# A third step for one product, its sums in places of their own, and idle passes on a constant

## The chip, the cores and the metric

The kernel runs on one core of a Trainium2 chip. The metric is the time of one execution in device microseconds (us), all in fp32. A profile is one execution recorded by the hardware. Engines: PE is TensorE (PEld its weight loads), DVE is VectorE, ACT is ScalarE, POOL is GpSimd, SP is SyncE (which here only issues DMAs).

## The reference

The input x is 8 sequences of 256 tokens with 1024 features. Two steps follow each other, each adding its result to x:

```
logits = x . Wr^T + 5 * onehot(language id)      # 8 experts
gates  = softmax over the two largest logits, 0 elsewhere
x = x + x . W^T + 2 * sum over experts e of gate_e * (x . A_e^T) . B_e^T    # rank 16
x = x + x . weight[adapter id of the sequence]^T                             # 1024 x 1024
```

The first step's base product x . W^T is 2048 tokens by 1024 by 1024. The second step is one 1024 x 1024 product for each sequence, with a weight chosen by its id.

## The kernel before

**Products by Winograd's scheme.** The base product is cut 2 x 2: features into halves of 512, outputs into halves of 512, tokens into halves of 1024. Seven block products named "1", "2", "5", "6", "3", "7", "4" (in the order in which they run) take the place of eight. Each block product is cut 2 x 2 again, into the products P1 to P7: sums S1 to S4 of weight blocks (128 x 512) and T1 to T4 of token blocks (128 x 1024) are made on DVE, and PE multiplies them. P1 and P6 collect in the PSUM tile A, P5 in B, P2 in X; P7 goes to A, P3 to B, P4 to A again. Such a product is four matmuls of 128 x 512.

**The third step.** Where `leaves` names them, P2, P3 or P4 are cut 2 x 2 once more (`third`, L439): seven matmuls of 128 x 256, and small sums r1 to r4 (128 x 128) and q1 to q4 (128 x 256) on DVE. Pieces 2, 3 and 4 collect straight in the product's own PSUM tile, pieces 1, 5, 6 and 7 in PSUM of their own, from where DVE takes them (`take`, L496) and adds them to the result. `place` says where the small sums lie: 0 is a pool of tiles, 1 and 2 are inside block 11 of x once it is dead, 3 is a stretch of the result block y12 that isn't in use yet.

**Product 2**, the one in question, has the third step for P2 and P4, not for P3. S4 and T4 overwrite S2 and T2, so they wait until PE has read these (P6). P3 (L821 and L823) is S4 times a block of x, added into B in two parts, with pieces of P4 between them.

**What sets the order.** The order is written out by hand for the opening and planned by `product` (L712) for the rest. The planner keeps two clocks, `now["pe"]` and `now["dve"]`, which it advances by estimated costs (`us`, L364: elements plus 66 over 960). Optional DVE steps wait in `queue` with the events that they need; `ahead` (L379) runs those that fit before a given time, `force` (L396) runs one that is needed now with all that stand before it. Each engine runs its instructions in the order in which they are issued, so a DVE step that stands earlier delays all later ones.

**Around the change.** After the opening (product 1), PE does 64 small matmuls, `project` (L251), 128 x 136: the down-projection and the logits of the second half of the tokens. DVE meanwhile makes the gates of the first half (`gating(0)`, L293: a chain of small steps over 128 x 64, in which most need the one before), multiplies them onto h, transposes the result (`turn`, L327) and sends it off: twelve DMAs on SP's queue and four copies on POOL, into `hg`. Then come S1, T1, the logits of one quarter, S2, T2, six small sums of P2 and S3, T3. POOL copies a few elements of hg (L1088, so that it waits for those DMAs) and then issues four DMAs that add x11 onto x12 and x12 onto x22. Product 2 follows, and while it runs DVE does the second half's gates, its turn, and S1, T1, S2, T2 of product 5.

**Opening.** PE begins with `WARM` idle matmuls of 128 x 128 (L592) on the identity matrix that POOL makes; their result isn't used. The first real matmuls (L601) need one 128-row piece each of W and x.

Of the kernel before, what the change touches and what calls it, by code (L numbers as in the profile page):

```python
# [16 lines left out]
P = 128  # L17
# [1 line left out]
LANG_BIAS = 5.0  # L19
SCALING = 2.0  # L20
NEG = -3.0e38
WARM = 6


@with_exitstack
def kernel(
# [31 lines left out]
    nc = tc.nc  # L58
    D = O = 1024
    E = NE  # L60
    ER = awT.shape[2] - E
# [8 lines left out]
    TQ = TH // 2  # L70
# [18 lines left out]
    def flat(blk):  # L89
        return blk.rearrange("p k n -> p (k n)")  # L90
# [144 lines left out]
    def minus(out_, x, y):  # L235
        tt(out_, x, y, ALU.subtract)
# [127 lines left out]
    def us(n):  # L364
        return (n + 66) / 960
# [73 lines left out]
    def third(key, leaf, lhs, rhs, place, what):  # L439

        ra = lambda i, j: lhs()[:, j, ts(i, P)]
        rb = lambda i, j: rhs()[:, i, ts(j, NQ)]
        n0, n1 = slice(0, NQ), slice(NQ, TQ)
        t, own = {}, {}
        at = {"r13": 0, "r2": P, "r4": 2 * P, "q13": 3 * P, "q2": 3 * P + NQ, "q4": 3 * P + 2 * NQ}
        me = f"{key}:L{leaf}"

        def op(name, tag, fn, x, y, what):  # L450
            width = P if name[0] == "r" else NQ

            def run():
                if place == 0:
                    t[name] = sub3.tile([P, width], F32, name=f"{name}_{key}{leaf}", tag=tag)
                elif place == 3:
                    t[name] = flat(yb["12"])[:, 2048 + at[tag] : 2048 + at[tag] + width]
                else:
                    t[name] = spare(1536 + (place - 1) * 1152 + at[tag], width)
                fn(t[name], *(t[v] if isinstance(v, str) else v() for v in (x, y)))  # L460

            return us(width), what, f"{me}.{name}", run

        A, B = (lambda i, j: lambda: ra(i, j)), (lambda i, j: lambda: rb(i, j))
        ops = [
            op("r1", "r13", add, A(1, 0), A(1, 1), what),
            op("q1", "q13", minus, B(0, 1), B(0, 0), what),
            op("r2", "r2", minus, "r1", A(0, 0), what),
            op("q2", "q2", minus, B(1, 1), "q1", what),
            op("r4", "r4", minus, A(0, 1), "r2", what),  # L470
            op("q4", "q4", minus, B(1, 0), "q2", what),
        ]
        ops3 = [
            op("r3", "r13", minus, A(0, 0), A(1, 0), (f"{me}.5", f"{me}.r2")),
            op("q3", "q13", minus, B(1, 1), B(0, 1), (f"{me}.5", f"{me}.q2")),
        ]

        def piece(n, acc=None, banks=None, fresh=False):
            if n in (1, 5):
                own[n] = (single(f"P{n}_{key}{leaf}", n // 5) if banks is None else banks[n // 5])[:, n0]  # L480
            for x in {3: ("r4",), 4: ("q4",), 5: ("r1", "q1"), 6: ("r2", "q2", "P1"), 7: ("r3", "q3", "P6")}.get(n, ()):
                force(f"{me}.{x}")
            out_, l, r = {
                1: lambda: (own[1], ra(0, 0), rb(0, 0)),
                2: lambda: (acc[:, 0, n0], ra(0, 1), rb(1, 0)),
                3: lambda: (acc[:, 0, n1], t["r4"], rb(1, 1)),
                4: lambda: (acc[:, 1, n0], ra(1, 1), t["q4"]),
                5: lambda: (own[5], t["r1"], t["q1"]),
                6: lambda: (own[1], t["r2"], t["q2"]),
                7: lambda: (own[1], t["r3"], t["q3"]),  # L490
            }[n]()
            nc.tensor.matmul(out_, lhsT=l, rhs=r, start=(n in (1, 5) or fresh and n in (2, 4)), stop=True, skip_group_check=True)  # L492
            now["pe"] += 0.432
            event(f"{me}.{n}", 0.2)

        def take(n, dest, base=None, sub=False):  # L496

            cut = lambda v: {1: v[:, 0, n0], 6: v[:, 0, n1], 5: v[:, :, n1]}[n]
            if n == 7:
                cut = lambda v: v[:, 1, :].rearrange("p (j n) -> p j n", j=2)  # L500
            src = own[5 if n == 5 else 1]
            if n in (5, 7):
                src = src.unsqueeze(1).to_broadcast([P, 2, NQ])
            evict(NQ if n in (1, 6) else TQ, cut(dest), src, None if base is None else cut(base), f"{me}.P{n}", sub)

        return ops, ops3, piece, take

    def make_subs(key, w, x, leaves=(), what=(), last=(), place=0, early=False):

# [11 lines left out]
        def op(name, fn, x, y, what):  # L523
# [10 lines left out]

            return us(2 * width), what, f"{key}.{name}", run

        late = [
            (us(2 * OQ), (f"{key}:P6",), f"{key}.s4", lambda: minus(t["s2"], a(0, 1), t["s2"])),
            (us(2 * TQ), (f"{key}:P6",), f"{key}.t4", lambda: minus(t["t2"], b(1, 0), t["t2"])),
        ]  # L540
        deep = {}
        if 2 in leaves:
            deep[2] = third(key, 2, lambda: a(0, 1), lambda: b(1, 0), 0, leaf2)
        if 3 in leaves:
            deep[3] = third(key, 3, lambda: t["s2"], lambda: b(1, 1), 1, (f"{key}:P6",))
        if 4 in leaves:
            deep[4] = third(key, 4, lambda: a(1, 1), lambda: t["t2"], 3 if early else 2, (f"{key}:P6",))
        subs[key] = (a, b, t, late, deep)
        return [
            op("s1", add, a(1, 0), a(1, 1), what),  # L550
# [37 lines left out]
    def opening(key, dest):  # L588


        idle = pair("idle", 2)
        for i in range(WARM):  # L592
            nc.tensor.matmul(idle[:, 0, :P], lhsT=ident, rhs=ident, start=True, stop=True)  # L593
        mm = multiply()
        ops = make_subs(key, "11", "11")
        sums_of = [ops[i][3] for i in range(6)]
# [46 lines left out]
        for o in ops3:  # L643
            vec(o[0], o[3], o[2])
        late[0][3]()
        next_leaf = third(key, 3, lambda: t["s2"], lambda: b(1, 1), 3, ())
        for o in next_leaf[0]:
            vec(o[0], o[3], o[2])
        late[1][3]()
# [25 lines left out]
        chunk(1)  # L675
        piece(6)
        out(6, q1, q1)
        next_leaf = third(key, 4, lambda: a(1, 1), lambda: t["t2"], 0, ())
        for o in next_leaf[0]:
            vec(o[0], o[3], o[2])  # L680
        chunk(2)
# [30 lines left out]
    def product(key, base, dest, lora=None, tokens=None, sub=False, joined=None):  # L712
# [22 lines left out]
        own = list(deep[2][1]) if 2 in deep else []  # L735
        own += late[:1] + (deep[3][0] if 3 in deep else []) + late[1:] + (deep[4][0] if 4 in deep else [])
        own += (deep[3][1] if 3 in deep else []) + (deep[4][1] if 4 in deep else [])
        rest = list(queue)
        queue[:] = [q for q in rest if q[2].startswith(key)] + own + [q for q in rest if not q[2].startswith(key)]
        A = new("A")  # L740
# [49 lines left out]
        join(3)  # L790
        if 4 in deep:
            _, _, piece4, take4 = deep[4]
            piece4(1)
            take4(1, at[2], old[2], sub)
        if 3 in deep:
            hold[0] = key
            _, _, piece, take = deep[3]
            force(f"{key}.X2")
            piece(1, banks=halves(X))
            take(1, at[1], at[1], sub)  # L800
            force(f"{key}.B5")
            mm(B, None, None, False, "d", 1, part=())
            piece(5, banks=halves(X))
            if 4 in deep:
                piece4(5)
            piece(6)
            take(6, at[1], at[1], sub)
            if 4 in deep:
                piece4(6)
                take4(6, at[2], old[2], sub)  # L810
            for n in (2, 3, 4):
                piece(n, B)
            piece(7)
            take(7, at[1], at[1], sub)
            take(5, at[1], at[1], sub)
            if 4 in deep:
                force(f"{key}.A7")
                mm(A, None, None, False, "1", 0, part=())
        elif 4 in deep:
            need("s4", "B5")  # L820
            mm(B, t["s2"], b(1, 1), False, "d", 1, ms=(0,))  # L821
            piece4(5)
            mm(B, t["s2"], b(1, 1), False, "d", 1, ms=(1,))  # L823
            piece4(6)
            take4(6, at[2], old[2], sub)
        else:
            need("s4", "B5")
            mm(B, t["s2"], b(1, 1), False, "d", 1)
        put(1, B, True, "B3")
        join(1)  # L830
        if 4 in deep:
            if 3 not in deep:
                force(f"{key}.A7")
                mm(A, None, None, False, "1", 0, part=())
            for n in (2, 3, 4):
                piece4(n, A)
            piece4(7)
            take4(7, at[2], old[2], sub)
            take4(5, at[2], at[2], sub)
            put(2, A, True, "A4")  # L840
        else:
            need("t4", "A7")
            mm(A, a(1, 1), t["t2"], False, "1", 0)
            put(2, A, name="A4")
        join(2)
        hold[0] = ""
# [221 lines left out]
    add_w("21", "22")  # L1068
    add_w("11", "21")
    done.clear()  # L1070
    now["pe"], now["dve"] = 0.0, 6.0
    event("S2", 16.0)
    after(0.4, lambda: take(0, 1))
    for i, (t, f) in enumerate(gating(0)):
        vec(t, f, "gates0")
    project(1, 0, halves(pair("ps_h_1_0", 2)))
    now["pe"] += 7.5
    subs2 = make_subs("2", "12", "21", (2, 4), early=True)
    run(subs2[:2])
    after(0.4, lambda: take(1, 0))  # L1080
    run(subs2[2:])
    project(1, 1, singles("ps_h_1_1"))
    now["pe"] += 7.5
    force("gates0")
    after(0.4, lambda: take(1, 1))

    landed = const.tile([ER, 4], F32, name="landed")
    nc.gpsimd.tensor_copy(landed, hg[0][:, :, 0, 0])  # L1088
# [107 lines left out]
```

## Time and profile before

| | |
|---|---|
| Median of 3 runs | 421.59 us (421.51 to 422.34) |
| The profiled execution's own time | 421.75 us |
| Its span, first to last instruction | 420.0 us |
| PE busy | 415.0 us, 99% |
| DVE busy | 307.7 us, 73% |
| POOL busy | 31.0 us, 7% |
| Product 2's first and next product's first matmul | 58.30 and 88.38 us |
| Last instructions' DMA issue | 416.97 us |

Times inside the profile count from the span's start. A row of a timeline has the start, the duration of the merged group, engine, line, operation, output and input names, shapes and count; in brackets stands how long the engine sat idle before it and what released it. One fp32 matmul leaves two records of PE and two of PEld, so x8 are four matmuls. A DVE row's duration is longer than the distance to the next row by about 0.08 us, because the next step begins while the last one drains.

### The profile page before, as it was taken

How to read it: one execution, taken by the hardware profiler on the slowest of the kernel's cores; microseconds unless marked ns; L12 is line 12 of the kernel's file. 1: busy time of each engine (PE TensorE's matmuls, PEld its weight loads, DVE VectorE, ACT ScalarE, POOL GpSimd, SP SyncE). 2: the span in 40 equal slices, each digit the busy share in tenths (PEclk: the TensorE clock that was granted, in tenths of full speed). 3: DMA queues.
4: the chain of work that ended last, by engine and by line, in shares of the span. 5: the costliest groups of instructions: out<-in, count | busy, mean ns of one | idle time of the engine just before them, and what ended most of it. 6: DMA issues, size and time to landing. Idle time of an engine off the chain costs nothing.

```text
span 420.0 us, 3774 instructions
## 1 busy us (share of the span) xinstructions
PE 415.0 (99%) x1314; PEld 231.2 (55%) x1314; DVE 307.7 (73%) x507; ACT 44.5 (11%) x75; POOL 31.0 (7%) x43
## 2 busy tenths in 40 slices
PE   8999999999999999999999999999999999999996
PEld 6679975455655556555565444444444444444574
DVE  1877688999668998999989876765657666665531
ACT  1120310122130000000000101010101101010110
POOL 2000232131011101102000000000000000000000
PEclk9999999999999999999999999999999999999999
DMA  8995567997992965938902492855568384640202
GB/s 287 381 395 243 103 127 146 205 184 229 244 225 28 193 194 95 247 61 157 336 8 100 162 334 105 282 215 204 206 202 293 113 316 171 234 166 2 100 0 100
DMA packets 22563, 77.61 MB, mean 185 GB/s; under 512 B 2064, under 2 KB 5136, under 8 KB 17552
## 3 DMA queue, kind: packets, MB, share of 16 engines
q1 hardware_dynamic: 16240, 59.66, 39.8%
q0 software_dynamic: 5056, 16.78, 21.7%
q10 hardware_dynamic: 1248, 0.93, 0.7%
q8 instruction: 10, 0.16, 0.2%
q14 instruction: 9, 0.07, 0.0%
HBM read 55.61 MB, written 8.39 MB: 152 GB/s over the span
## 4 chain that ended last, share of the span: by engine, by line
PE 99%; POOL 0%; ACT 0%; issue 0%; POOLq 0%
PE A L944 23%; PE A L576 19%; PE B L944 13%; PE B L576 11%; PE ps_h L259 7%; PE X L944 7%; PE P L492 6%; PE A_last L1011 3%; PE X L492 3%; PE X L576 3%; PE A L492 2%; PE B L492 2%; PE idle L593 1%; ACT z L1041 0%; PE ids_wide L620 0%
## 5 line engine op out<-in xcount | busy, mean ns | idle before, releaser
L576 PE MATMUL A<-t,s 128*128 128x512 f32 x112 | 50.3, 592 | 0.0
L944 PE MATMUL B<-x,x 128*128 128x512 f32 x96 | 43.2, 592 | 0.0
L944 PE MATMUL A<-w,x 128*128 128x512 f32 x88 | 39.6, 592 | 0.0
L944 PE MATMUL A<-w,y 128*128 128x512 f32 x88 | 39.1, 592 | 0.0
L259 PEld LDWEIGHTS ps_h<-y,x 128*128 128x128 f32 x256 | 31.7, 190 | 2.9 <-issue 2.5
L576 PEld LDWEIGHTS A<-t,s 128*128 128x128 f32 x112 | 21.2, 190 | 20.8 <-issue 20.1
L259 PE MATMUL ps_h<-y,x 128*128 128x136 f32 x256 | 31.9, 279 | 0.0
L230 DVE TENSOR_TENSOR y<-P,y 128x512 f32<-128x512 f32 (+1 forms) x41 | 23.3, 570 | 10.8 <-PE P L492 5.7
L944 PEld LDWEIGHTS B<-x,x 128*128 128x128 f32 x96 | 18.2, 190 | 22.1 <-issue 22.0
L230 DVE TENSOR_TENSOR w<-w,w 128x1024 f32<-128x1024 f32 x16 | 19.4, 1224 | 13.5 <-PE A L944 13.5
L944 PEld LDWEIGHTS A<-w,x 128*128 128x128 f32 x88 | 16.7, 190 | 21.0 <-issue 20.8
L944 PEld LDWEIGHTS A<-w,y 128*128 128x128 f32 x88 | 16.7, 190 | 20.6 <-issue 20.6
L576 PE MATMUL A<-x,w 128*128 128x512 f32 x56 | 25.3, 592 | 0.0
L230 DVE TENSOR_TENSOR y<-A,y 128x1024 f32<-128x1024 f32 x18 | 22.0, 1223 | 4.2 <-PE A L576 2.9
L230 DVE TENSOR_TENSOR x<-w,x 128x1024 f32<-128x1024 f32 (+1 forms) x13 | 11.1, 863 | 10.8 <-PE A L944 7.8
L227 ACT ACTIVATE z<-A 128x512 f32<-128x512 f32 x12 | 7.2, 597 | 101.0 <-PE A L944 101.0
L230 DVE TENSOR_TENSOR w<-x,w 128x1024 f32<-128x1024 f32 x8 | 9.7, 1224 | 10.2 <-PE A L944 5.7
L576 PEld LDWEIGHTS A<-x,w 128*128 128x128 f32 x56 | 10.4, 190 | 9.8 <-issue 9.6
L230 DVE TENSOR_TENSOR x<-x 128x1024 f32<-128x1024 f32 (+1 forms) x17 | 15.8, 947 | 0.0
L230 DVE TENSOR_TENSOR y<-X,y 128x256 f32<-128x256 f32 (+2 forms) x17 | 12.8, 752 | 3.8 <-PE X L492 3.3
L230 DVE TENSOR_TENSOR z<-z,X 128x512 f32<-128x512 f32 x7 | 4.8, 689 | 13.6 <-PE X L944 13.6
L944 PE MATMUL X<-w,y 128*128 128x512 f32 x32 | 14.4, 592 | 0.0
(200 smaller groups left out, 612.3 us busy)
## 6 DMA issues: line engine op xcount, KB each, us to landing
x<-w_dram SPq DMA_DIRECT2D x24, 1024.0 KB, 4.8
x<-xT_dram SPq DMA_DIRECT2D x10, 1024.0 KB, 11.8
w<-w_dram SPq DMA_DIRECT2D x8, 1024.0 KB, 4.8
out_dram<-z SPq DMA_DIRECT2D x15, 512.0 KB, 2.9
w<-w POOLq DMA_DIRECT2D x8, 512.0 KB, 5.3
x<-x POOLq DMA_DIRECT2D x4, 1024.0 KB, 9.8
x<-xT_dram POOLq DMA_DIRECT2D x4, 1024.0 KB, 11.4
y<-y POOLq DMA_DIRECT2D x8, 512.0 KB, 5.1
```

Of the source, the lines that this page charges most:

```text
L227: nc.scalar.activation(out_, x, AF.Copy, scale=scale)
L230: nc.vector.tensor_tensor(out_, x, y, op)
L259: nc.tensor.matmul(ps[v][:, u * EA : (u + 1) * EA], lhsT=xk(k, j, c)[:, ts(r, P)], rhs=aw_sb[:, k, :], start=(first and k == some[0] and u ...
L492: nc.tensor.matmul(out_, lhsT=l, rhs=r, start=(n in (1, 5) or fresh and n in (2, 4)), stop=True, skip_group_check=True)
L576: nc.tensor.matmul(acc[:, m, :], lhsT=l, rhs=r, start=(first and i < len(ms)), stop=(i >= len(steps) - len(ms)), skip_group_check=True,)
L593: nc.tensor.matmul(idle[:, 0, :P], lhsT=ident, rhs=ident, start=True, stop=True)
L944: nc.tensor.matmul(accs[name], lhsT=lhs[:, k // 2, k % 2, :], rhs=rhs[:, k, :], start=(first and k == 0), stop=(k == KH - 1), skip_group_c ...
L1011: nc.tensor.matmul(acc, lhsT=lhs[:, k // 2, k % 2, :], rhs=rhs[:, k, ts(v, m)], start=(first and k == 0), stop=(k == KH - 1), skip_group_c ...
```

## The change

The change has four parts.

1. Product 2 gets the third step for P3 too (`leaves` (2, 3, 4)). P3's piece 1 and piece 5 go to the two halves of X, after X has been read out.
2. Its S4 and T4 no longer overwrite S2 and T2: S4 lies in y12, T4 in y22 (`apart`). So they don't wait for P6, nor do P4's six small sums, and T4, these sums and S4 are now made ahead of the product, right after the last logits. P3's small sums get a new place 4, in gaps of y12.
3. P2's six small sums move from behind T2 to between the first steps of the first half's gates, one after each step. The second half's gates are no longer held back in the last part of product 2 (`hold` isn't set for it).
4. The idle matmuls read a constant 1.0 (one element for each partition, read over and over) that the program's preamble sets, and there are seven in place of six.

```diff
-WARM = 6
+WARM = 7
...
+                elif place == 4:
+                    to = {"r13": 3712, "r2": 3840, "r4": 3968, "q13": 1664, "q2": 0, "q4": NQ}[tag]
+                    t[name] = flat(yb["12"])[:, to : to + width]
...
-    def make_subs(key, w, x, leaves=(), what=(), last=(), place=0, early=False):
+    def make_subs(key, w, x, leaves=(), what=(), last=(), place=0, early=False, apart=None):
...
-        late = [
-            (us(2 * OQ), (f"{key}:P6",), f"{key}.s4", lambda: minus(t["s2"], a(0, 1), t["s2"])),
-            (us(2 * TQ), (f"{key}:P6",), f"{key}.t4", lambda: minus(t["t2"], b(1, 0), t["t2"])),
-        ]
+        def op4(name, x):
+
+            old, width = ("s2", OQ) if name == "s4" else ("t2", TQ)
+
+            def run():
+                if apart is None:
+                    t[name] = t[old]
+                else:
+                    t[name] = apart[name].rearrange("p (k n) -> p k n", k=2)
+                minus(t[name], x, t[old])
+
+            return us(2 * width), (f"{key}:P6",) if apart is None else (), f"{key}.{name}", run
+
+        late = [op4("s4", a(0, 1)), op4("t4", b(1, 0))]
+        what4 = (f"{key}:P6",) if apart is None else ()
...
-            deep[3] = third(key, 3, lambda: t["s2"], lambda: b(1, 1), 1, (f"{key}:P6",))
+            deep[3] = third(key, 3, lambda: t["s4"], lambda: b(1, 1), 4 if early else 1, what4)
...
-            deep[4] = third(key, 4, lambda: a(1, 1), lambda: t["t2"], 3 if early else 2, (f"{key}:P6",))
+            deep[4] = third(key, 4, lambda: a(1, 1), lambda: t["t4"], 3 if early else 2, what4)
...
+        one = nc.const_aps.tensor(1.0, [P, P])
         for i in range(WARM):
-            nc.tensor.matmul(idle[:, 0, :P], lhsT=ident, rhs=ident, start=True, stop=True)
+            nc.tensor.matmul(idle[:, 0, :P], lhsT=one, rhs=one, start=True, stop=True)
...
+        own = [q for q in own if q[2] not in done]
...
+            need("t4")
             piece4(1)
...
-            hold[0] = key
+            if key != "2":
+                hold[0] = key
             _, _, piece, take = deep[3]
-            force(f"{key}.X2")
+            need("s4", "X2")
             piece(1, banks=halves(X))
...
-    now["pe"], now["dve"] = 0.0, 6.0
+    now["pe"], now["dve"] = 0.0, 3.5
     event("S2", 16.0)
     after(0.4, lambda: take(0, 1))
-    for i, (t, f) in enumerate(gating(0)):
-        vec(t, f, "gates0")
     project(1, 0, halves(pair("ps_h_1_0", 2)))
     now["pe"] += 7.5
-    subs2 = make_subs("2", "12", "21", (2, 4), early=True)
+    apart2 = {"s4": flat(yb["12"])[:, 3200:3712], "t4": flat(yb["22"])[:, : C * ER]}
+    subs2 = make_subs("2", "12", "21", (2, 3, 4), early=True, apart=apart2)
+    small2, subs2[4:10] = subs2[4:10], []
+    for t, f in gating(0):
+        vec(min(t, 0.16) if t < 0.5 else t, f, "gates0")
+        run([small2.pop(0) for _ in small2[:1]])
     run(subs2[:2])
     after(0.4, lambda: take(1, 0))
     run(subs2[2:])
...
-    force("gates0")
     after(0.4, lambda: take(1, 1))
+    _, _, _, (s4, t4), deep2 = subs["2"]
+    run([t4] + deep2[4][0] + [s4])
```

The other products' calls only change the name under which S4 and T4 are found; they still lie on S2 and T2.

More of the change, by code (lines that the diff above doesn't have):

```diff
@@ L645, in opening @@
         late[0][3]()
-        next_leaf = third(key, 3, lambda: t["s2"], lambda: b(1, 1), 3, ())
+        next_leaf = third(key, 3, lambda: t["s4"], lambda: b(1, 1), 3, ())
         for o in next_leaf[0]:
@@ L677, in opening @@
         out(6, q1, q1)
-        next_leaf = third(key, 4, lambda: a(1, 1), lambda: t["t2"], 0, ())
+        next_leaf = third(key, 4, lambda: a(1, 1), lambda: t["t4"], 0, ())
         for o in next_leaf[0]:
@@ L820, in product @@
             need("s4", "B5")
-            mm(B, t["s2"], b(1, 1), False, "d", 1, ms=(0,))
+            mm(B, t["s4"], b(1, 1), False, "d", 1, ms=(0,))
             piece4(5)
-            mm(B, t["s2"], b(1, 1), False, "d", 1, ms=(1,))
+            mm(B, t["s4"], b(1, 1), False, "d", 1, ms=(1,))
             piece4(6)
@@ L827, in product @@
             need("s4", "B5")
-            mm(B, t["s2"], b(1, 1), False, "d", 1)
+            mm(B, t["s4"], b(1, 1), False, "d", 1)
         put(1, B, True, "B3")
@@ L842, in product @@
             need("t4", "A7")
-            mm(A, a(1, 1), t["t2"], False, "1", 0)
+            mm(A, a(1, 1), t["t4"], False, "1", 0)
             put(2, A, name="A4")
```

## The prediction

> **What bounds the kernel now.** I read the page's busy table and its chain first. In both, columns are engine, time and share.
>
> ```profile
> PE 415.0 (99%) x1314; PEld 231.2 (55%) x1314; DVE 307.7 (73%) x507; ACT 44.5 (11%) x75; POOL 31.0 (7%) x43
> ...
> PE 99%; POOL 0%; ACT 0%; issue 0%; POOLq 0%
> ```
>
> TensorE (PE) is busy for 415.0 of 420.0 us and carries the whole chain. So time goes only with matmuls removed, with a slow clock ended sooner, or with a PE wait removed; it comes only with a new PE wait. The view of PE's waits has a single line, at the very start:
>
> ```profile
> PE idle L593 <- POOL ident masks.py:199: 1.5, 1, 1.5
> ```
>
> Next, PE's timeline of the first ten us (start, duration, instruction, count; one fp32 matmul leaves two records), and the landing times of the two loads issued first, at 0.75 (last column: us from issue to landing):
>
> ```profile
> 1.53 2.93 PE L593 MATMUL idle<-ident 128*128 128x128 f32 x12 [1.53 <-POOL ident masks.py:199]
> ...
> 4.25 2.97 PE L576 MATMUL X<-x,w 128*128 128x512 f32 x4
> ...
> 7.06 1.09 PE L259 MATMUL ps_h<-y,x 128*128 128x136 f32 x8
> ...
> 7.98 1.88 PE L576 MATMUL X<-x,w 128*128 128x512 f32 x4
> ```
>
> ```profile
> x<-xT_dram SPq DMA_DIRECT2D x1, 256.0 KB, 3.1
> w<-w11T_dram ACTq DMA_DIRECT2D x1, 128.0 KB, 3.3
> ```
>
> The same two matmuls take 7.06-4.25 = 2.81 us at first and 9.70-7.98 = 1.72 us afterwards (the next group starts at 9.70): 1.09 us are lost to half speed. Half speed loses half its time, so it lasted some 2.2 us after 4.25, to about 6.43, which is 4.9 us after the first idle pass at 1.53. The two loads land at 0.75+3.1 = 3.85 and 0.75+3.3 = 4.05; the first real weight load starts at 4.06.
>
> Last, product 2 on PE, at the place of its P3 (78.92 and 81.93 are P3's four matmuls; P4's pieces stand between):
>
> ```profile
> 78.49 0.59 PE L492 MATMUL P<-t,w 128*128 128x256 f32 x2
> 78.92 1.88 PE L576 MATMUL B<-x,s 128*128 128x512 f32 x4
> 80.64 1.02 PE L576 MATMUL B<-hg,bdiff 128*128 128x512 f32 x2
> 81.50 0.59 PE L492 MATMUL P<-y 128*128 128x256 f32 x2
> 81.93 1.88 PE L576 MATMUL B<-x,s 128*128 128x512 f32 x4
> 83.64 1.02 PE L576 MATMUL B<-hg,bdiff 128*128 128x512 f32 x2
> ```
>
> **Part 1: P3 in seven pieces.** It removes four 128x512 matmuls, 1.72 (78.92 to 80.64) + 1.71 (81.93 to 83.64) = 3.43 us, and adds seven 128x256 ones at 0.433 (81.50 to 81.93) = 3.03 us. The low-rank matmuls stay. PE gains 0.40 us, if nothing waits.
>
> **Part 2: what it costs VectorE (DVE).** P3's pieces need eight small sums, 4 x (0.20+0.34) = 2.1 us, and four more reads out of PSUM, 0.33+0.33+0.73+0.64 = 2.0 us. DVE had room: it idles 1.95 us before 64.08, and 0.68 us twice more (before 68.02 and 75.26). The question is whether every step stays ahead of PE, so I lay the new order (as the built program has it) out with the start-to-start times of these rows: a 128x1024 step 1.14, 128x512 0.60, 128x256 0.34, 128x128 0.20; a gate step 0.26 when it needs the one before, 0.14 when it doesn't (two in 0.30 at 49.62).
>
> ```profile
> 49.62 0.30 DVE L230 TENSOR_TENSOR y<-y 128x64 f32<-128x64 f32 x2
> ...
> 61.90 0.24 DVE L230 TENSOR_TENSOR y<-ps_h,bias 128x16 f32<-128x16 f32 x2
> 64.08 0.42 DVE L230 TENSOR_TENSOR y<-P,y 128x256 f32<-128x256 f32 x1 [1.95 <-PE P L492]
> ```
>
> First gates: six steps took 1.55 (47.04 to 48.59); with a small sum between each they take 6 x 0.14 + 1.62 = 2.46. Up to T2 all is 0.9 us later; then the six small sums (1.61, 58.55 to 60.16) are missing, so the pair at 61.90 comes at 61.20 and DVE is free at 61.37. The 0.9 us delay is covered: S2 and T2, done at 59.6, are read on PE at 64.31. It also moves the first turn's twelve DMAs on SP and four copies on POOL, and behind them in POOL's queue the wait for their landing (65.06, now 66.0) and the four adds onto x12 and x22. PE first reads the turned gates at 69.90, 3.9 us later. The first add onto x12 landed before 73.1 (POOL issues the next one then), now 74.0; product 5's T1 reads it at 81.7 at the earliest. Nothing there costs time.
>
> From 61.37: T4 1.14, P4's six sums 1.62, S4 0.60 and 0.12 for its end: 64.84. Two sums of P3 0.54, the P1 read of P2 0.33, its r3 and q3 0.54, four sums of P3 1.08: 67.33. Seven second-gate steps 1.68, A6 1.14, a P6 read 0.33, gates up to the exponential and past it 1.35+0.53: 72.36. B5 1.14, four gate steps 0.73, gates onto h 1.14, P7 and P5 reads 1.45: 76.82. X2 1.14, the transpose 1.17, A7 1.14, P4's first read 0.33: 80.61, and P3's first read ends at 81.02. On PE, P3's first piece follows P4's at 78.92 and needs X2 (ends 78.05): no wait. After two low-rank matmuls P3's second piece is due at 81.07, and in the built order it waits for that read at 81.02: it just fits, with 0.05 us to spare. What hides all this is 0.05 us of slack; every 0.1 us that DVE is later there is 0.1 us on the end, and behind the waiting piece stands all of PE.
>
> Two costs are not in that sum. First, POOL's copies for the second turn:
>
> ```profile
> 83.38 3.07 POOL L338 COPY hg<-y 32x256 f32<-32x256 f32 x4 [4.40 <-DVE y L330]
> 83.41 0.64 DVE L230 TENSOR_TENSOR y<-t 128x256 f32<-128x256 f32 x1
> 83.97 0.88 DVE L230 TENSOR_TENSOR x<-w 128x512 f32<-128x512 f32 x1
> 84.77 1.41 DVE L230 TENSOR_TENSOR x<-x 128x1024 f32<-128x1024 f32 x1
> 86.11 0.41 DVE L230 TENSOR_TENSOR y<-P,y 128x256 f32<-128x256 f32 x1
> ```
>
> While POOL copies, a sum of two SBUF tiles is 0.2 us longer (1.41 for 1.22, 0.88 for 0.68); the read from PSUM at 86.11 is not. The copies now come at about 79.9 (behind the fourth add on POOL, 78.12 plus the 0.9 of delay and its 0.86) and cover product 5's S1 and T1: 80.94, 81.74, 83.08; then r3 0.20, two P6 reads 0.67 and q3, which ends at 84.36. PE's P7 of P3 waits for it and is due at 81.07 + 7 x 0.433 = 84.10: 0.26 us of stall; without contention q3 ends at 83.96 and there is none. Second, A7 and two reads from PSUM also lie beside these copies. The Trainium skill ("SBUF — State Buffer", "Who interferes with whom") says that a VectorE step with at most one SBUF input doesn't contend with GpSimd. The trace has only the small read at 86.11 for it, near the copies' end; should A7 and the reads be slower as the SBUF sums are (0.2 + 0.1 + 0.1), 0.4 us of stall follow. I take 0, with row and rule. Third, the exit: product 5's B is due at 92.24-0.40 = 91.84 and needs A4, which the same layout ends at 91.4 to 91.9: no more than what is counted. Part 2 costs 0.25, between 0 and 0.7. Parts 1 and 2: -0.15 us (-0.4 to +0.3).
>
> **Part 3: the idle passes.** They no longer wait for the identity (1.47), only for the engines' common start; DVE and SP begin at 0.75 to 0.83, so I take 0.85. Seven passes of 0.42 (the twelve records' starts) end at 3.8: the first real matmul stays bound by its load at 4.05. The gain is only in when full speed is granted. By the row, 4.9 us after the first pass: 5.75 for 6.43, worth 0.68/2 = 0.34 us. The Trainium skill speaks against taking that as fixed: "TensorE: Matmul & The Clock Gate" ("What's actually happening") has a free-running window of about 3.4 us at whose end a busy window opens the clock. By it, the grant comes 3.4 to 6.8 us after the first pass: half speed on real work costs 0.45 to 2.15 us before and 0.1 to 1.8 after; the mean gain is again 0.34, but one run may move by over 1 us either way. The times shown (421.51 to 422.34, 0.83 apart) look like that. I take the -0.34 of the row, and the spread of the rule for the range. With windows ending at 3.01 and 6.43 as in this profile, PE was busy for 1.5 us of the one that ends at 3.01, now 2.2: should that suffice, all 1.09 is gained. At the other end the grant stays where it is: 0.
>
> **Sum.** -0.15-0.34 = -0.5 us. The profiled execution took 421.75 (span 420.0 plus 1.75 around it), the median is 421.59: 421.25 and 421.1, so I say 421.2. A measurement tells about 0.2% (0.84 us) from no change, so the likeliest outcome is a gain too small to be told.
>
> **Rivals.** (a) The clock opens a window earlier, or DVE just fits everywhere: -0.4 to -0.15 and -1.09 make 420.1 to 420.5, and combinations of half of it end near 420.7. For it: the first window is now 64% busy. Against: 43% were not enough before. 0.30. (b) It doesn't do what it says: the grant stays and the stalls eat the 0.40: 421.5 to 421.8. 0.20. (c) Slower: DVE is late at P3's second piece. If small sums between gates don't fill the gaps (0.26 a gate step for 0.14: 0.7 us), and PSUM reads contend (0.4), the read ends at 82.1, PE stalls 1.05, and 0.25 more at P7: 421.7-0.4+1.3 = 422.6. From 0.4 us of lateness on, the change costs time. For it: a margin of 0.05 after 20 us of unbroken DVE work. Against: the step times repeat to 0.01 us. 0.12. The forecast has the other 0.38.
>
> **How the numbers follow.** Faster (below 420.75) is case (a), 0.30; slower (above 422.43) is (c), 0.12; same 0.58. The range, 420.3 to 422.1, takes in -1.3 (the early clock with a stall) and +0.4 (no clock gain, both contentions).
>
> **What would show it.** Right: idle passes from 0.85 with x14 records; the first X matmuls in 2.1 to 2.5 us rather than 2.81; seven 128x256 pairs of records in place of P3; DVE without idle from 61 to 91; at most one PE wait on DVE, under 0.3 us, at P3's P7. Wrong: a wait of 0.5 us or more at P3's second piece, a PE wait for DMA in the opening, a wait at product 5's B, or X matmuls as slow as before.

## The result and the profile after

The changed kernel takes 421.09 us (median of 22 runs, 420.25 to 421.55), the kernel before 421.62 us in as many runs beside it (420.77 to 422.44). The ratio is 0.9984, 95% interval 0.9978 to 0.9991: a gain of 0.4 to 0.9 us. It is clear of zero and, most likely, under 0.2%. The profiled execution took 421.29 us, with a span of 419.5 (421.75 and 420.0 before).

The page after, engines' busy time and the chain:

```profile
PE 415.3 (99%) x1322; PEld 232.7 (55%) x1322; DVE 310.1 (74%) x519; ACT 44.4 (11%) x75; POOL 29.6 (7%) x43
...
PE 99%; ACT 0%; issue 0%
```

PE is still the whole chain. Its busy time didn't fall, although P3 costs less: the idle passes now run for longer, and they count as busy. The view of PE's waits has again only the one at the start, which is now the engines' common start rather than the identity:

```profile
PE idle L608 <- PEq L1208: 0.8, 1, 0.8
```

PE's opening after (start, duration, group):

```profile
0.79 3.33 PE L608 MATMUL idle<-const-float32-1.0 128*128 128x128 f32 x14 [0.79 <-PEq L1208]
4.08 3.02 PE L590 MATMUL X<-x,w 128*128 128x512 f32 x4
6.94 1.09 PE L259 MATMUL ps_h<-y,x 128*128 128x136 f32 x8
```

The passes begin 0.74 us earlier, but the first two real matmuls take 6.94-4.08 = 2.86 us, as slow as before (2.81). In this one execution full speed was granted hardly earlier (at 6.21 us by the trace's record of the clock, 6.43 before); only the start moved. Product 2 after, from P3's first piece to the next product's first matmul:

```profile
78.80 0.59 PE L495 MATMUL X<-x,y 128*128 128x256 f32 x2
...
80.95 0.67 PE L495 MATMUL X<-y 128*128 128x256 f32 x2
81.46 0.59 PE L495 MATMUL P<-y 128*128 128x256 f32 x2
...
87.92 3.60 PE L590 MATMUL A<-x,w 128*128 128x512 f32 x8
```

Two pieces follow each other by 0.43 us everywhere but after 80.95, where it is 81.46-80.95 = 0.51: 0.08 us is waited at P3's second piece, the place that the prediction named. Product 2 takes 87.92-58.18 = 29.74 us, against 88.38-58.30 = 30.08: 0.34 us of gain. It also begins 58.30-58.18 = 0.12 us earlier. Together that is the whole difference of the two spans, because what follows product 5's first matmul takes 331.6 us in both (419.5-87.92, 420.0-88.38).

VectorE and POOL after: the first gates with P2's small sums between their steps, then the stretch from the last logits to product 5's sums:

```profile
46.92 0.22 DVE L286 TENSOR_REDUCE y<-y 128x8 f32<-128x64 f32 x1
47.06 0.28 DVE L230 TENSOR_TENSOR r<-w 128x128 f32<-128x128 f32 x1
...
61.10 0.24 DVE L230 TENSOR_TENSOR y<-ps_h,bias 128x16 f32<-128x16 f32 x2
...
79.02 1.19 DVE L230 TENSOR_TENSOR y<-A,y 128x1024 f32<-128x1024 f32 x1
...
80.46 0.41 DVE L230 TENSOR_TENSOR y<-X,y 128x256 f32<-128x256 f32 x1
80.79 0.67 DVE L230 TENSOR_TENSOR x<-w 128x512 f32<-128x512 f32 x1
81.38 1.22 DVE L230 TENSOR_TENSOR x<-x 128x1024 f32<-128x1024 f32 x1
```

```profile
79.16 1.69 POOL L338 COPY hg<-y 32x256 f32<-32x256 f32 x4
```

A gate step with a small sum behind it takes 47.06-46.92 = 0.14 us of VectorE's time, the forecast's figure. The logits' pair stands at 61.10 (61.90 before), and from there VectorE has no gap over 0.34 us. P3's first read ends at 80.87 and PE is due at 80.95: the fit that the layout promised (81.02 for 81.07, with everything 0.12 us earlier here), and yet PE waits 0.08 us. POOL's copies came at 79.16 and end at 80.85, just as S1 of product 5 (80.79) begins.

### The profile page after: what moved, and what is told of

The parts are those of the page before. It is cut to its first block, busy times and chain, and to the rows that moved or that the text cites. A ratio compares the mean times of both kernels' runs of the same rounds, so it can differ in the third digit from the quotient of the medians.

```text
span 419.5 us, 3804 instructions
## 1 busy us (share of the span) xinstructions
PE 415.3 (99%) x1322; PEld 232.7 (55%) x1322; DVE 310.1 (74%) x519; ACT 44.4 (11%) x75; POOL 29.6 (7%) x43
## 4 chain that ended last, share of the span: by engine, by line
PE 99%; ACT 0%; issue 0%
PE A L962 23%; PE A L590 19%; PE B L962 13%; PE B L590 10%; PE ps_h L259 7%; PE X L962 7%; PE P L495 6%; PE X L495 4%; PE A_last L1029 3%; PE X L590 3%; PE A L495 2%; PE B L495 2%; PE idle L608 1%; ACT z L1059 0%; PE ids_wide L635 0%
## 5 line engine op out<-in xcount | busy, mean ns | idle before, releaser
L230 DVE TENSOR_TENSOR y<-X,y 128x256 f32<-128x256 f32 (+2 forms) x21 | 15.0, 715 | 3.8 <-PE X L495 3.3
L962 PE MATMUL X<-x,y 128*128 128x512 f32 x32 | 14.4, 592 | 0.0
```

The costliest lines, as they stand in the source:

```text
L230: nc.vector.tensor_tensor(out_, x, y, op)
L962: nc.tensor.matmul(accs[name], lhsT=lhs[:, k // 2, k % 2, :], rhs=rhs[:, k, :], start=(first and k == 0), stop=(k == KH - 1), skip_group_c ...
```

## The experiments

My theory was the prediction's: P3's pieces give 0.40 us less what PE waits for VectorE, and the idle passes give about 0.34 us on average by an earlier grant of full speed, with a large scatter from run to run. The rivals were that one of the two carries everything, and that VectorE has room enough for the order not to matter. Ratios are to the kernel before, run on the same chip. It took 421.49 us (44 runs) beside the passes alone, the first measurement of P3 without the passes, the sums behind T2 and the last experiment, and 421.78 us (48 runs) beside the others, so compare ratios from one experiment to the next, not microseconds.

**The idle passes alone.** To the kernel before:

```diff
-WARM = 6
+WARM = 7
...
+        one = nc.const_aps.tensor(1.0, [P, P])
         for i in range(WARM):
-            nc.tensor.matmul(idle[:, 0, :P], lhsT=ident, rhs=ident, start=True, stop=True)
+            nc.tensor.matmul(idle[:, 0, :P], lhsT=one, rhs=one, start=True, stop=True)
```

> The kernel before with the idle passes of the change alone (seven, on the constant). Theory: the earlier passes open the clock earlier by their head start on average, 0.7 us, worth 0.34 us: ratio 0.9992 (0.9985 to 1.0000), single runs over 1 us apart. In the profile: passes from 0.79, no new wait on PE, product 2's first matmul at 57.7 to 58.6. Rival (the profile of the changed kernel, where the grant came only 0.22 us earlier): 0.11 us, ratio 0.9997. Rival (all of the gain is P3): 1.0000.

Measured: 421.07 us in 13 runs, ratio 0.9991 (0.9983 to 0.9999). So the passes give some time. How much, the interval leaves open: it holds the theory's 0.34 us and the rival's 0.11. PE's opening in this kernel's profile:

```profile
4.13 2.02 PE L576 MATMUL X<-x,w 128*128 128x512 f32 x4
6.00 1.09 PE L259 MATMUL ps_h<-y,x 128*128 128x136 f32 x8
```

Here the two matmuls take 1.87 us rather than 2.86: nearly all of the half speed was over before real work began. From product 2's to product 5's first matmul it is 87.32-57.24 = 30.08 us, as before.

**P3 without the passes.** To the changed kernel, the passes of before (six, on the identity).

> The changed kernel with the idle passes of before (six, on the identity). Theory: only P3's seven pieces are left, 0.40 us less the 0.08 us of wait at P3's second piece: 0.32 us under the kernel before, ratio 0.9992. From product 2's first to product 5's first matmul: 29.74 us, as in the changed kernel (30.08 before). Rival (P3 carries the whole measured gain): 0.67 us, ratio 0.9984. Rival (the idle passes carry all): 1.0000.

Measured: 421.43 us in 14 runs, ratio 0.9997 (0.9988 to 1.0006), which holds both the theory and "nothing". The profile has product 2 at 87.91-58.24 = 29.67 us. A second measurement of the same kernel, with more runs:

> The changed kernel with the old idle passes, once more with five rounds, because the first measurement (ratio 0.9997, 0.9988 to 1.0006) couldn't tell the theory from its rival. Theory: what its profile shows in product 2 (29.67 us for 30.08) is all there is, 0.40 us, ratio 0.9990. Rival (product 2's gain is given back later): 1.0000.

Measured: 421.34 us in 22 runs, ratio 0.9988 (0.9982 to 0.9995). The two measurements, weighed by their intervals, make about 0.9991 (0.9986 to 0.9996; an estimate of mine), some 0.4 us. The profiles settle it: product 2 takes 29.68 us in this one too (88.80-59.12), and what follows product 5's first matmul takes 331.58 to 331.61 us in all profiles of this document but that of P3's pieces alone. So P3's pieces give time of their own, and "given back later" falls. The opening of this second profile is the slowest of all that have idle passes:

```profile
4.42 3.63 PE L590 MATMUL X<-x,w 128*128 128x512 f32 x4
7.88 1.09 PE L259 MATMUL ps_h<-y,x 128*128 128x136 f32 x8
```

The two matmuls take 3.46 us, although the passes stand where they stood before.

**No idle pass at all.** To the changed kernel, `WARM = 0`.

> The changed kernel without any idle pass. Theory (a window of 3.4 us at a free phase, so a grant 3.4 to 6.8 us after PE's first work, and here that is the first real matmul at 4.05): half speed lasts 3.4 to 6.8 us of real work and costs 1.7 to 3.4 us, against 0.1 to 1.7 with the passes: slower than the changed kernel by about 1.6 us, 422.7, ratio to the kernel before 1.0025 (1.0015 to 1.004). Rival (the grant comes near 6 us whatever PE did before, as four of the profiles have it at 5.7 to 6.4): no change against the changed kernel, ratio 0.9985.

Measured: 422.63 us in 17 runs, ratio 1.0022 (1.0014 to 1.0029). By the ratios that is 1.6 us over the changed kernel (0.9984). The theory's figure holds, the fixed moment falls. The first matmul waits for its load and then four records take 3.78 us where 1.88 is the full pace:

```profile
4.36 3.78 PE L590 MATMUL X<-x,w 128*128 128x512 f32 x4 [4.36 <-DMA w<-w11T_dram]
```

**The small sums behind T2.** To the changed kernel:

```diff
-    small2, subs2[4:10] = subs2[4:10], []
+    small2 = []
```

> The changed kernel with product 2's six small sums back behind T2 instead of between the first gates. Theory: VectorE reaches T4 0.7 us later (six gate steps at 0.26 for 0.14) and nothing gives that back, so the wait at P3's second piece grows from 0.08 to 0.6 to 0.8 us: slower than the changed kernel by 0.5 to 0.7, that is 421.7, ratio to the kernel before 1.0000 (0.9995 to 1.0008). Rival (the 0.7 us are absorbed in gaps of VectorE before 81, at A6, B5 or the exponential): no more than 0.2 us over the changed kernel, ratio 0.9987.

Measured: 421.81 us in 13 runs, ratio 1.0007 (0.9999 to 1.0016). PE now waits long enough for VectorE that its timeline marks it:

```profile
79.03 1.88 PE L590 MATMUL B<-hg,bdiff 128*128 128x512 f32 x4
81.40 0.70 PE L495 MATMUL X<-y 128*128 128x256 f32 x2 [0.49 <-DVE y L230]
81.93 0.59 PE L495 MATMUL P<-y 128*128 128x256 f32 x2
```

The piece was due at 79.03+1.72 = 80.75, and the next one starts at 81.93, so it began to stream at 81.50: 0.75 us of wait (the row's 0.49 leaves out the time until the group before is modelled to end). Product 2 takes 88.40-57.98 = 30.42 us, 0.68 more than with the sums between the gates. T4 begins 0.67 us later, counted from product 2's first matmul (61.74-57.98 for 61.27-58.18), and nothing on VectorE gave that back; without this move P3's pieces cost more than they save.

**S4 and T4 in place.** To the changed kernel:

```diff
-    subs2 = make_subs("2", "12", "21", (2, 3, 4), early=True, apart=apart2)
+    subs2 = make_subs("2", "12", "21", (2, 3, 4), early=True)
...
-    _, _, _, (s4, t4), deep2 = subs["2"]
-    run([t4] + deep2[4][0] + [s4])
```

> The changed kernel with S4, T4 and P4's sums back on S2 and T2 and behind P6 (P3's seven pieces, the sums between the gates and the idle passes stay). Theory: VectorE's gap at 62 to 64 us is filled by the second gates instead, which don't have to wait, so only dependent gate steps (0.26 for 0.14) and one wait are lost: the wait at P3's second piece is 0.3 to 0.5 us instead of 0.08, product 2 takes 30.0 to 30.2 us, time 421.3 to 421.5, ratio to the kernel before 0.9992. Rival (S4 and T4 behind P6 leave the gap unused and cost its 1.95 us): 422.9, ratio 1.0035.

Measured: 421.43 us in 13 runs, ratio 0.9996 (0.9988 to 1.0004). Product 2 takes 88.02-57.75 = 30.27 us, just above what I expected, because there are two waits:

```profile
80.71 0.70 PE L495 MATMUL X<-y 128*128 128x256 f32 x2
81.24 0.59 PE L495 MATMUL P<-y 128*128 128x256 f32 x2
...
84.04 0.70 PE L495 MATMUL X<-y 128*128 128x256 f32 x2
84.58 1.88 PE L590 MATMUL A<-hg,b_sb 128*128 128x512 f32 x4
```

The first is at P3's second piece, 0.29 us (streaming from 81.24-0.43 = 80.81, due at 80.52). The second is at P7, 0.32 us (from 84.15, due at 83.83), where I had expected none. It is the stall that the prediction had worked out for the changed kernel. Here POOL's copies do run into product 5's sums:

```profile
79.35 3.50 POOL L338 COPY hg<-y 32x256 f32<-32x256 f32 x4
```

```profile
81.16 1.42 DVE L230 TENSOR_TENSOR x<-x 128x1024 f32<-128x1024 f32 x1
82.51 0.48 DVE L230 TENSOR_TENSOR y<-s 128x128 f32<-128x128 f32 x1
```

T1 and r3 are 0.2 us longer each (1.22 and 0.29 in the changed kernel), so q3 ends at 83.99, and P7 streams 0.16 us after it. By this sum, without these 0.4 us P7 would not have waited (83.59+0.16 for 83.83). The gap at 62 us is filled by the second half's gates, as the theory said; the rival's 1.95 us don't appear.

**P3's pieces alone.** To the kernel before: the third step for P3 of product 2, the new place for its sums, and `hold` not set for it; nothing else.

```diff
+                elif place == 4:
+                    to = {"r13": 3712, "r2": 3840, "r4": 3968, "q13": 1664, "q2": 0, "q4": NQ}[tag]
+                    t[name] = flat(yb["12"])[:, to : to + width]
...
-            deep[3] = third(key, 3, lambda: t["s2"], lambda: b(1, 1), 1, (f"{key}:P6",))
+            deep[3] = third(key, 3, lambda: t["s2"], lambda: b(1, 1), 4 if early else 1, (f"{key}:P6",))
...
-            hold[0] = key
+            if key != "2":
+                hold[0] = key
...
-    subs2 = make_subs("2", "12", "21", (2, 4), early=True)
+    subs2 = make_subs("2", "12", "21", (2, 3, 4), early=True)
```

> The kernel before with P3's seven pieces alone (their sums in the new place 4, gates not held back): S4, T4 and all small sums at their old moments, old idle passes. Theory: VectorE, not PE, then sets product 2's end. Laid out with the step times of the trace, product 5's S1 and T1 come only at 92 to 94 us, so product 5's B, due at 91.8, waits some 2.1 us, and its P5 0.5 us more: 0.40 gained, 2.6 lost, 423.7 us, ratio 1.005 (1.004 to 1.007). Rival (VectorE's idle 3.3 us in product 2 take the 4.1 us of new work, stall under 0.8 us at P3's own pieces): ratio 1.0000 to 1.0010.

Measured: 436.15 us in 4 runs, ratio 1.0339 (1.0324 to 1.0354). The side was right, the size wrong by 12 us. PE's waits:

```profile
PE B L579 <- DMA hg<-y: 9.9, 1, 9.9
PE B L579 <- DVE x L230: 1.9, 1, 1.9
```

The 1.9 us at product 5's B are those that I had worked out. What I hadn't followed are the second half's turned gates. On VectorE their transpose comes at 90.90 (82.07 in the kernel before, 77.86 in the changed one). On POOL their copies stand behind a DMA that waits 6.3 us for a load, but they are over at 105.20. The twelve DMAs go out from 92.16 on and take SP until 108.95; for them PE stands still for 9.9 us until 112.32. Why they went out so slowly (1.3 us each in the median on SP, 0.6 for the first half's before) is not shown. After such a pause it has lost full speed as well: the trace's record of the clock has no full speed from 106.8 to 117.06, and the four matmul records from 112.32 take 3.75 us in place of 1.88. Behind product 2 this profile has 15.2 us more than the kernel before: waits of 9.9, 1.9 and 0.3 us and half of 4.7 us of slow work make 14.4, and the rest is time that the rows of these waits leave out, as at 81.40 above. Less 0.4 us for the pieces that is 14.8 us in this execution, the slowest of the four; the medians lie 14.4 apart (421.78 us beside it). A further wait of 0.4 us for VectorE, at PE's tile A, lies in the opening; the part on the idle passes takes it up.

**One more step.** To the changed kernel: in product 2, P4's fifth piece stands ahead of P3's fifth instead of behind it.

```diff
-            piece(5, banks=halves(X))
-            if 4 in deep:
+            if 4 in deep and key == "2":
+                piece4(5)
+            piece(5, banks=halves(X))
+            if 4 in deep and key != "2":
                 piece4(5)
             piece(6)
```

> The changed kernel with P4's fifth piece ahead of P3's fifth piece in product 2 alone. Theory: the wait at P3's second piece (0.08 us) is covered by the 0.43 us of P4's piece, so no wait is left on PE in product 2 and its length is 29.66 us instead of 29.74: 0.08 us under the changed kernel, which the times can't tell, but the profile can. Rival (the wait only moves to P3's sixth piece, or to P7): length stays at 29.74.

Measured: 420.74 us in 14 runs, ratio 0.9982 (0.9973 to 0.9991).

```profile
80.83 0.59 PE L495 MATMUL P<-y 128*128 128x256 f32 x2
81.26 1.03 PE L495 MATMUL X<-y 128*128 128x256 f32 x4
```

All pieces now follow by 0.43 us, and product 2 takes 87.72-58.06 = 29.66 us. It is the fastest version of the study, under the kernel before for sure. That it beats the changed kernel is not shown: the two intervals overlap, and with the changed kernel's order product 2 takes 29.74, 29.67, 29.68 and 29.73 us in four profiles (the changed kernel, the old passes twice, no passes), so the wait of 0.08 us isn't in every execution.

## Why the prediction was right, point by point

**P3 in seven pieces: 0.40 us.** Right. The profile has 0.34 with 0.08 of wait, the step above shows 0.42 without it, and the kernel with the old passes gains about 0.4 us by its runs (0.15 to 0.6, both measurements together). The kernel with the passes alone keeps 30.08.

**VectorE's layout.** Right to 0.1 us over 20 us: P3's first read ends at 80.87 where 81.02-0.12 was due. The slack was not right. The read is over 0.08 us before the piece is due, more than the 0.05 forecast, and PE waits all the same: from the read's end to the piece's first streaming 0.16 us pass (80.87 to 81.46-0.43 = 81.03). The pieces that wait in two other profiles show the same, 81.35 to 81.50 with the sums behind T2 and 80.65 to 80.81 with S4 and T4 in place. The layout had put this handover at nothing; with it, its 0.05 us to spare are a wait of 0.11. The sums behind T2 show what a step without slack means: 0.7 us later at T4 became 0.68 us on product 2.

**The contention with POOL: 0.25 us of the 0.25 for Part 2.** For this kernel the term was wrong in its time, not in its mechanism. I put the copies at 79.9 to 83.0, as long as in the profile before (3.07 us). They began at 79.16, because the fourth add stood at 78.25 on POOL and not at 79.0: the first half's turned gates, on which the adds wait, landed at 65.18 (65.06 before) although their transpose came 0.83 us later (53.66 for 52.83). What took up that delay is not shown. And the copies took 1.69 us, since nearly all that VectorE did beside them (A7, 1.19 us, and small reads) had one operand in PSUM. S1 and T1 took their plain 0.67 and 1.22, and P7 waited for nothing. With S4 and T4 in place the copies met S1 and T1 after all, and P7 waited 0.32 us, near the forecast 0.26. The row for it was there: the copies of 3.07 us had themselves been slowed by the SBUF sums beside them. Instead 0.08 us came at the second piece.

**Product 5's entry.** Right: B starts at 91.79 with no wait.

**The idle passes: 0.34 us.** The mean agrees with the runs, which give 0.04 to 0.7 us for the passes alone; the single profile doesn't: 0.22 us earlier, worth 0.11. "X matmuls as slow as before" was the prediction's own sign of being wrong here, and this profile has it (2.86 us). By the trace's record of the clock, full speed came this long after PE's first work:

| Kernel | First work, us | Granted, us | Between | Product 2 begins, us |
|---|---|---|---|---|
| before | 1.53 | 6.43 | 4.90 | 58.30 |
| old passes | 1.53 | 6.13 | 4.60 | 58.24 |
| old passes, again | 1.53 | 7.75 | 6.22 | 59.12 |
| P3 alone | 1.52 | 4.42 | 2.90 | 58.30 |
| changed | 0.79 | 6.21 | 5.42 | 58.18 |
| passes alone | 0.79 | 4.25 | 3.46 | 57.24 |
| sums behind T2 | 0.79 | 5.80 | 5.01 | 57.98 |
| one more step | 0.79 | 5.72 | 4.93 | 58.06 |
| S4, T4 in place | 0.79 | 5.08 | 4.29 | 57.75 |
| no passes | 4.36 | 8.66 | 4.30 | 59.53 |

The delay lies between 2.9 and 6.2 us, 4.6 on average, wherever the first work stands. That is a spread of 3.3 us, what the Trainium skill's free-running window of 3.4 us would give ("TensorE: Matmul & The Clock Gate", "What's actually happening"). The traces agree on the window: by their record of the clock, full speed lasts 413.01 us in seven of them, 416.43 in two, and 102.40 and 317.44 on either side of the pause with P3 alone, with 10.24 of half speed between. All are whole multiples of 3.413 us (121, 122, 30, 93 and 3).

But the shortest delay, 2.9 us, is under one window, so a window that was not busy from its start sufficed. Counted back from the grant, it began at 1.00, with PE at work from 1.52, for about 80% of it. In the second profile with the old passes a window from 0.93 to 4.34, in which six passes of 0.43 us fill about 75%, did not suffice. Both shares are my estimates.

A later grant costs half of what it is later: product 2's start less half the grant is 55.1 to 55.2 us in nine of the ten rows, with grants from 4.25 to 8.66. The tenth, P3 alone, shows when an early grant is worth nothing. It has 56.1: VectorE got pieces of W and x there at 10.78 and 12.49, where the passes alone, with the clock nearly as early, had them at 9.80 and 11.24. PE then waited for VectorE until 17.18 (the 0.4 us at A) and lost the gain.

So a head start of 0.74 us should move the mean grant by that much and the mean time by half of it, 0.37 us, where the loads keep up. One profile of each kernel, with a spread of 3.3 us, can't show such a shift, and the runs bound it only as said.

**The sum.** The profile's 0.46 us for the forecast 0.5 is in part luck: P3's pieces brought 0.08 us of wait, not 0.25, and in this execution the clock gave 0.12 us, not 0.34. The two errors nearly cancel.

**The chances.** Case (a), the early clock and all that goes with it, happens in some executions (passes alone, 4.25 us), not in the median. Its reason, a first window that is now 64% busy, did not hold in the changed kernel's profile: the window that ended at 6.21-3.41 = 2.80 had PE at work from 0.79, 59% of it, and the grant came one window later. With the passes alone a window happened to begin at 0.83, just behind the first pass. The slower case needed 0.4 us of lateness; with the sums between the gates there were 0.08.

## What to carry to other kernels

When PE carries the whole chain, a cheaper product is worth its matmuls only if the engine that feeds it keeps up, so lay that engine's new order out step by step up to each place where PE waits; here 0.7 us of order decided between gain and loss. Follow what a late step sends off as well: with P3's pieces alone VectorE's own lateness cost PE 1.9 us, the DMAs of the gates that it sent off late 9.9. A start-up effect with a free phase must be judged by many runs, because one profile draws only one value of it; and an early start pays only if the loads behind it keep up.

## What the runs showed of the hardware

Interleaving independent small sums into a chain of dependent 128x64 steps shortens each such step from 0.26 to 0.13 us of VectorE's time (47.26 to 47.39; 0.14 at 46.92). POOL's copies and VectorE's two-operand SBUF sums slow each other (copies 3.07 to 3.50 us, sums 0.2 us longer each); beside reads from PSUM the same copies took 1.69 us. From the end of a VectorE read to the first streaming of the matmul that waits for it 0.15 to 0.16 us passed in three profiles. A pause of PE of 9.9 us lost full speed, which came back 4.7 us after work resumed.
